# One fused comparison in the dilation, and later transposes in the first GraphSAGE layer

## The chip, the cores and the metric

The kernel runs on one core of one Trainium2 chip. The metric is the device time of one execution in microseconds, as the median of several runs. In the views of the profile PE is TensorE (PEld its weight loads), DVE is VectorE, ACT is ScalarE, POOL is GpSimd and SP is SyncE, which here only issues DMAs.

## What is computed

Two graph layers, each on `relu(layernorm(x))` and added back to x, for B = 16 graphs of N = 1024 nodes with D = 128 features and a sparse symmetric adjacency with weights.

The first layer is attention with 8 heads over the neighbours. The second is three GraphSAGE layers over an adjacency that has been dilated first. The dilation goes through the rows in order, and what a row removes is gone for the rows behind it:

```
def step(carry, n):
    row = jnp.take(carry, n, axis=0)
    nbi = row.astype(jnp.int32)
    num = jnp.sum(nbi)
    sf = jnp.where(num > T_DIL, (num + K_DIL - 1) // K_DIL, 1)   # T_DIL = 10, K_DIL = 2
    rank = jnp.cumsum(nbi)
    rm = row & (rank % sf == 0)
    valid = (mask_b[n] != 0) & (num > 1)
    rm = jnp.where(valid, rm, False)
    keep = ~rm
    carry = carry.at[n].set(row & keep)
    carry = carry.at[:, n].set(carry[:, n] & keep)
    return (carry, None)
```

So a row with more than ten neighbours loses those of rank sf and (where there is one) 2 sf, a row of two to ten neighbours loses all of them, and a row of at most one (or a masked one) loses none. Each GraphSAGE layer is

```
deg = jnp.clip(jnp.sum(adj, axis=-1, keepdims=True), 1.0, None)
out = (jnp.einsum('bij,bjd->bid', adj, x) / deg) @ Wr + x @ Wx + b
out = out / jnp.maximum(jnp.linalg.norm(out, axis=-1, keepdims=True), NORM_EPS)
```

followed by relu and a batch norm over all graphs and nodes; the three layers' results go through one last linear map.

## The kernel before, in words

The program has two stages, one after the other. The order of the instructions of PE, ACT and DVE is the order in which the program text issues them; the DMA queues of SP and POOL are ordered by the scheduler.

**Attention, with the dilation beside it** (about 2315 us). Attention is a loop over 256 turns: 16 graphs, two halves c of 512 query nodes, eight blocks m of 128 key nodes. Each turn has two half steps g (four heads each). One half step does, on PE, the scores of the heads (L554 puts in the mask, L560 the products), then the weighted sums of the half step before (L487, L492); on ACT two exponentials over 128x1024 (L598); on DVE two products with the weights of the adjacency over 128x1024 (L603). Around this the turn transposes a piece of the adjacency (L505 on PE, copied by L508 and made a mask by L512 on ACT), and small steps prepare the next graph and conclude the last (L288 to L432).

The dilation is a generator whose pieces are put between the half steps by planned costs (`beside_attention`). It takes eight blocks k of 128 rows, all 16 graphs at a time. Each block first finds, in seven rounds, which neighbours of the diagonal square are removed (L743 to L847). It then has for each row of the block and each graph the number of neighbours, from which it makes per row the thresholds `th` (L851 to L865). At the end of the block comes a loop over the graphs, `for i in range(B + 2)` (L896), with one graph entering at each i, and its steps set apart by one i each. In this text "row" means one graph of this loop: a tile of 128 rows by 1024 columns. For one graph it does

- i: the sums of pairs along the row on DVE (L900), kept once for two columns, then on ACT two activations `wr = |2 sum + at|` (L915), one for the even and one for the odd columns, each 128x512 in f16, with `at_even` or `at_odd` as a bias per partition;
- i + 1: on DVE, a column is removed where `wr == off`, and everywhere if `allof` says that the row loses all (L924, two operations of 512 columns that write every second column of `er`), times the row (L928); then the removals found by earlier blocks are put in (L930, over the columns before the block);
- i + 2: on PE eight transposes of `er` (L907), copied on ACT (L909); ACT reads the next block's row of this graph (L699, L703); DVE joins the diagonal square (L937) and takes the removed columns out of the next block's row (L716, over the columns before the block); SP writes rows and columns of the removals `mr_d` to HBM and loads `ad`, `gm` and `gl` for later rows.

One graph takes two half steps of attention. The buffers are `wr` 2, `er` 3, `et` 2, `pair_sums` 2.

**GraphSAGE** (from about 2315 us). A loop over three layers L, 16 graphs b and two halves c. A turn reads its half of the transposed adjacency (`aT`, 2 MB) and the removals (`mr`) that were fetched some turns ahead, and DVE has put the one into the other (L146) during the turn before. On PE it does the nodes' own part (L1118), then four pieces "sums" of 16 records each (L1132), into one PSUM tile. The result of the turn before is finished between these pieces: DVE scales it (L1150), ACT squares it (L1155), DVE and ACT make the norm, DVE the normalised `o` (L1165), PE transposes `o` (L1169), ACT copies the transposed tile (L1173), DVE takes the statistics (L1176). Where the transposes stand is set by `turn_later` (L1288): without it they come after the second of the four pieces, with it after the third. In the kernel before it holds for the first halves (c = 0) but the first one of a layer; the second halves (c = 1) have the transposes after the second piece.

Of the kernel before, what the change touches and what calls it, by code (L numbers as in the profile page):

```python
# [34 lines left out]
def swept(ctx: ExitStack, tc: tile.TileContext, t: dict, out: bass.AP, flag: bass.AP):  # L35
# [131 lines left out]
    def first_part(p1):  # L167
# [483 lines left out]
        def dilation():  # L651
# [9 lines left out]
            def rk(b, lo, hi):  # L661
                return rks[b // (B // 2)][:, b % (B // 2), lo:hi]
# [73 lines left out]
            for k in range(NB):  # L736
# [112 lines left out]


                th = small.tile([P, 5, B], F32, name=f"th_{k}", tag="th", bufs=2)  # L851
                num, at_odd, off, allof, at_even = (th[:, i, :] for i in range(5))
                high = v[:, 3, :]
                nc.vector.tensor_tensor(mosts, most, gone[:, B : 2 * B], ALU.subtract)
                nc.vector.tensor_tensor(num, mosts, gone[:, :B], ALU.subtract)
                nc.vector.tensor_tensor(changed[:, k * B : (k + 1) * B], num, prev, ALU.not_equal)
                nc.vector.tensor_scalar(high, num, 10.5, None, ALU.is_gt)
                nc.vector.scalar_tensor_tensor(allof, num, 1.5, high, ALU.is_gt, ALU.subtract)

                nc.vector.tensor_scalar(num, num, 0.5, 0.25, ALU.mult, ALU.add)  # L860
                nc.vector.tensor_scalar(num, num, MAGIC, MAGIC, ALU.add, ALU.subtract)
                nc.vector.tensor_scalar(at_odd, num, -3.0, None, ALU.mult)
                nc.vector.tensor_scalar(at_even, num, -3.0, 2.0, ALU.mult, ALU.add)
                nc.vector.scalar_tensor_tensor(off, num, 1.0, high, ALU.add, ALU.mult)
                nc.vector.tensor_scalar(off, off, -1.0, None, ALU.add)  # L865
                yield 2.0, 1

                nc.vector.tensor_tensor(in_pairs(valid), in_pairs(valid), over_rows(vb[:, 0]), ALU.mult)
# [27 lines left out]
                for i in range(B + 2):  # L896
                    b = i
                    if b < B:
                        row = rk(b, 0, N + 2)
                        nc.vector.tensor_tensor_scan(  # L900
                            pair_sums[b % 2], row[:, 0::2], row[:, 1::2], 0.0, ALU.add, ALU.add
                        )
                    b = i - 2
                    if 0 <= b:
                        pe = ps_d.tile([P, NB, P], BF, name=f"pe_{k}_{b}", tag="d")
                        for j in range(NB):
                            nc.tensor.transpose(pe[:, j, :], ers[b][:, j * P : (j + 1) * P], ident_bf)  # L907
                        ets[b] = pool.tile([P, NB, P], BF, name=f"et_{k}_{b}", tag="et", bufs=2)
                        nc.scalar.copy(ets[b], pe)  # L909
                    yield (1.3 if i < B else 0.0), "B"  # L910
                    b = i
                    if b < B:
                        wrs[b] = pool.tile([P, N], F16, name=f"wr_{k}_{b}", tag="wr", bufs=2)
                        for t, at in enumerate((at_even, at_odd)):
                            nc.scalar.activation(  # L915
                                wrs[b][:, t * HN : (t + 1) * HN], pair_sums[b % 2][:, t : t + HN], AF.Abs,
                                bias=at[:, b : b + 1], scale=2.0,
                            )
                    b = i - 1
                    if 0 <= b < B:  # L920
                        er = ers[b] = pool.tile([P, N], BF, name=f"er_{k}_{b}", tag="er", bufs=3)
                        wr = wrs.pop(b)
                        for t in range(2):
                            nc.vector.tensor_scalar(  # L924
                                er[:, t::2], wr[:, t * HN : (t + 1) * HN], off[:, b : b + 1], allof[:, b : b + 1],
                                ALU.is_equal, ALU.max,
                            )
                        nc.vector.tensor_tensor(er, er, rk(b, 2, N + 2), ALU.mult)  # L928
                        if k > 0:
                            nc.vector.tensor_tensor(er[:, :n0], er[:, :n0], gms.pop(b)[:, :n0], ALU.max)  # L930
                    known(i + 1)
                    b = i - 2
                    if 0 <= b:
                        if more:
                            read(k + 1, b)
                        er, et = ers.pop(b), ets.pop(b)
                        nc.vector.tensor_tensor(er[:, n0:n1], er[:, n0:n1], et[:, k, :], ALU.max)  # L937
                        nc.sync.dma_start(mr_d[b][:, k, :n1], er[:, :n1])
                        if k > 0:
                            nc.sync.dma_start(mr_d[b][:, :k, n0:n1], et[:, :k, :])  # L940
                        if more:
                            nc.sync.dma_start(mr_d[b][:, k + 1 :, n0:n1], et[:, k + 1 :, :])
                            if b >= 2:
                                survive(k + 1, b - 2)
                            fetch_removed(k + 1, b)
                    if more and i < B:
                        fetch(k + 1, i)
                    yield (2.9 if i < B else 1.2), ("A" if i < B + 1 else 1)
# [263 lines left out]
    with tc.manual_schedule(  # L1212
# [6 lines left out]
        for L in range(3):  # L1219
# [10 lines left out]
            for b in range(B):  # L1230
# [4 lines left out]
                for c in range(2):  # L1235
# [49 lines left out]
                            next(last_rows)  # L1285
                    if biased:
                        next(biased)
                    turn_later = before and c == 0 and b > 0  # L1288
                    if before and not turn_later:
                        go(before, "transposed")  # L1290
                    pieces[2]()
# [686 lines left out]
```

## Time and profile before

| what | value |
|---|---|
| median of 3 runs | 3405.87 us (3404.3 to 3407.48) |
| the profiled execution, its own time | 3404.63 us |
| its span, first to last instruction | 3402.8 us |
| mean granted clock of TensorE | 0.994 |
| PE, DVE, ACT busy | 97%, 89%, 68% of the span |
| DVE L603, products of attention | 1024 of 1219 ns |
| ACT L598, exponentials | 1024 of 1022 ns |
| DVE L900, pair sums | 128 of 1218 ns |
| ACT L915, `wr` | 256 of 730 ns |
| ACT L909, copies of the transposed removals | 128 of 994 ns |
| PE L1132, sums of GraphSAGE | 6144 of 275 ns |

A line of the profile's groups reads: line, engine, operation, written tile <- read tiles, shapes, count | busy time in us, mean of one in ns | idle time of the engine just before them, and what ended it. The timeline reads: start and duration in us, engine, line and operation, tiles and count; in brackets the idle time before it, and what ended that. A duration runs from an instruction's start to its end, and consecutive instructions of an engine overlap at their ends, so two of 1022 ns can take 1.94 us together. PE's records are pipelined, so that PE's idle time shows best as the distance between the starts of records.

### The profile page before, as it was taken

The numbers are of one execution on the slowest core, as the hardware profiler recorded it, in microseconds if no ns is written. First come the engines' busy times: TensorE is split into PE (matmuls) and PEld (weight loads), VectorE is DVE, ScalarE is ACT, GpSimd is POOL, SyncE is SP. The second block draws the span as 40 slices with busy tenths as digits, with TensorE's granted clock in tenths as the row PEclk, the third lists the DMA queues.
The fourth block names the chain that finished last, engine by engine and source line by source line (L and its number), as shares of the span: only waits on it lengthen the run. The fifth ranks groups of instructions, "written<-read, shape, count | busy, mean of one in ns | idle before, by whom it ended". The sixth has DMA issues, their size and how long they took to land. (4 is left out here: it accounts for less than half of the span.)

```text
span 3402.8 us, 86338 instructions
## 1 busy us (share of the span) xinstructions
PE 3312.8 (97%) x34855; PEld 1874.3 (55%) x34855; DVE 3023.9 (89%) x5399; ACT 2303.8 (68%) x3909; POOL 163.8 (5%) x253
## 2 busy tenths in 40 slices
PE   8999999999999999999999999999999899999997
PEld 3333333333333333333333334337999899999997
DVE  7898989989989999998998999997888799978887
ACT  7699689779879869968977986883222344423334
POOL 2000000000000000000000000000000000000000
PEclk9999999999999999999999999999999999999999
DMA  7357457547637646845854874677999799989996
GB/s 241 109 169 207 134 151 212 151 138 223 179 121 222 207 128 195 238 126 166 247 175 125 250 221 123 198 230 272 336 334 336 273 354 351 354 308 351 352 351 220
DMA packets 650123, 772.28 MB, mean 227 GB/s; under 512 B 173264, under 2 KB 569168, under 8 KB 637424
## 3 DMA queue, kind: packets, MB, share of 16 engines
q1 hardware_dynamic: 632672, 708.58, 64.3%
q0 software_dynamic: 15456, 57.30, 5.0%
q8 instruction: 275, 4.51, 0.6%
q14 instruction: 136, 1.11, 0.1%
q10 hardware_dynamic: 1584, 0.79, 0.1%
HBM read 508.50 MB, written 157.29 MB: 196 GB/s over the span
## 5 line engine op out<-in xcount | busy, mean ns | idle before, releaser
L603 DVE TENSOR_TENSOR w<-e,aT 128x1024 f32<-128x1024 f32 x1024 | 1205.4, 1219 | 136.4 <-ACT e L598 134.7
L598 ACT ACTIVATE e<-sc 128x1024 f32<-128x1024 f32 x1024 | 991.6, 1022 | 330.0 <-PE sc L560 329.8
L1132 PE MATMUL pg<-y,aT 128*128 128x128 f32 (+1 forms) x6144 | 732.2, 275 | 0.0
L1132 PEld LDWEIGHTS pg<-y,aT 128*128 128x128 f32 x6144 | 710.4, 192 | 0.0
L487 PE MATMUL acc<-w,both 128*32 128x512 f32 x4096 | 586.8, 605 | 1.2 <-DVE w L603 0.8
L560 PE MATMUL sc<-qT,kT 32*128 32x512 f32 x4096 | 584.1, 640 | 0.3 <-ACT qT L315 0.3
L492 PE MATMUL acc<-e,eps 128*32 128x512 f32 x4096 | 573.5, 592 | 0.0
L146 DVE SCALAR_TENSOR_TENSOR aT<-mr,aT 128x1024 f32<-128x1024 bf16 x384 | 458.9, 1217 | 0.0
L492 PEld LDWEIGHTS acc<-e,eps 128*32 128x32 f32 x4096 | 150.6, 110 | 294.6 <-issue 289.3
L1155 ACT ACTIVATE sq<-o 128x512 f32<-128x512 f32 x96 | 60.6, 631 | 357.8 <-DVE o L1150 357.8
L554 PEld LDWEIGHTS <-never 32*32 32x32 bf16 x8192 | 80.1, 88 | 344.3 <-issue 324.0
L554 PE MATMUL sc<-nomask,never 32*32 32x512 bf16 x8192 | 248.6, 385 | 16.0 <-ACT e L598 13.2
L1173 ACT COPY hT<-pt 128x512 f32<-128x512 f32 x96 | 56.2, 585 | 267.7 <-PE pt L1169 259.2
L560 PEld LDWEIGHTS sc<-qT,kT 32*128 32x128 f32 x4096 | 160.1, 183 | 116.9 <-issue 116.1
L505 PEld LDWEIGHTS pa<-ident,a 128*128 128x128 f32 x1024 | 107.8, 141 | 181.3 <-issue 131.2
L487 PEld LDWEIGHTS acc<-w,both 128*32 128x32 f32 x4096 | 92.9, 108 | 154.2 <-issue 65.1
L915 ACT ACTIVATE wr<-both,th 128x512 f16<-128x512 f16 x256 | 172.0, 730 | 7.1 <-DVE both L900 6.9
L505 PE MATMUL pa<-ident,a 128*128 128x128 f32 x1024 | 168.3, 287 | 6.6 <-DMA a<-in_adj 6.0
L512 ACT ACTIVATE nomask<-aT 128x512 bf16<-128x512 f32 x256 | 161.3, 630 | 8.1
L1150 DVE SCALAR_TENSOR_TENSOR o<-pg,rdeg,mine 128x128 f32<-128x128 f32 x384 | 108.2, 345 | 60.1 <-PE pg L1132 57.0
L900 DVE TENSOR_TENSOR_SCAN both<-rk 128x513 f16<-128x513 bf16 x128 | 155.9, 1218 | 0.0
L508 ACT COPY aT<-pa 128x512 f32<-128x512 f32 x256 | 152.8, 597 | 4.5 <-PE pa L505 4.5
(228 smaller groups left out, 3894.0 us busy)
## 6 DMA issues: line engine op xcount, KB each, us to landing
aT<-aT_d SPq DMA_DIRECT2D x94, 2048.0 KB, 9.8
mr<-mr_d SPq DMA_DIRECT2D x188, 512.0 KB, 6.0
aT_d<-aT SPq DMA_DIRECT2D x256, 256.0 KB, 4.0
a<-in_adj SPq DMA_DIRECT2D x253, 256.0 KB, 3.9
ad<-in_adj SPq DMA_DIRECT2D x112, 512.0 KB, 4.2
nomask<-nomask SPq DMA_DIRECT2D x512, 96.0 KB, 2.7
nomask<-nomask SPq DMA_DIRECT2D x512, 64.0 KB, 2.8
nomask<-nomask SPq DMA_DIRECT2D x512, 32.0 KB, 2.7
```

What stands on the lines that cost most here:

```text
L146: nc.vector.scalar_tensor_tensor(part, mrs[h][:, j : j + 2, :].rearrange("p j n -> p (j n)"), 0.0, part, ALU.is_equal, ALU.mult)
L487: nc.tensor.matmul(acc[g][32 * j : 32 * j + 32, :], v1[:, m, (2 * j + g) * HW : (2 * j + g) * HW + 32], ws[j // 2][:, j % 2, :], start=(m ...
L492: nc.tensor.matmul(acc[g][32 * j : 32 * j + 32, :], eps8, es[j // 2][:, j % 2, :], start=False, stop=(m == NB - 1),)
L505: nc.tensor.transpose(pa[:, k * P : (k + 1) * P], a[:, k, :], ident)
L512: nc.scalar.activation(nomask[:, 0, :], aT[:, 0, :], AF.Relu, bias=1.0, scale=-1e38, accum_out=zeros[:, i : i + 1])
L554: nc.tensor.matmul(scs[j // 2][to : to + 32, j % 2, :], never[rows, rows], nomask[rows, j, :], start=True, stop=False, tile_position=(32 * ...
L560: nc.tensor.matmul(scs[j // 2][:, j % 2, :], kT[rows, mm], qTs[c][rows, g, :], start=False, stop=True, tile_position=(32 * j, 0),)
L598: nc.scalar.activation(e, scs[q], AF.Exp, scale=1.0 / math.sqrt(HD))
L603: nc.vector.tensor_tensor(w, es[q], aT.to_broadcast([P, 2, HN]), ALU.mult)
L900: nc.vector.tensor_tensor_scan(pair_sums[b % 2], row[:, 0::2], row[:, 1::2], 0.0, ALU.add, ALU.add)
L915: nc.scalar.activation(wrs[b][:, t * HN : (t + 1) * HN], pair_sums[b % 2][:, t : t + HN], AF.Abs, bias=at[:, b : b + 1], scale=2.0,)
L1132: nc.tensor.matmul(pg[:, i // 2, at : at + width], aT[:, j, i * P : (i + 1) * P], y[:, j, :width], start=(j == 0), stop=(j == NB - 1),)
```

## The change

Two independent parts, one in the dilation and one in the GraphSAGE loop.

In the dilation the two comparisons and the product with the row become one `scalar_tensor_tensor`: `(wr == off) * row`, over both halves, read and written with a step of two elements. The maximum with `allof` is gone. A row that loses all its neighbours is made to compare equal everywhere instead: a new threshold `twos` is 2 for the others and 0 for such a row, it becomes the scale of the two activations (a column of 128 values where the constant 2 was), and `at_odd`, `at_even` and `off` are made from it, so that such a row has `wr = 0 = off`. The thresholds take one small operation more per block.

In the GraphSAGE loop `turn_later` holds for the second halves of the first layer (L = 0) too.

```diff
-                num, at_odd, off, allof, at_even = (th[:, i, :] for i in range(5))
+                num, at_odd, off, twos, at_even = (th[:, i, :] for i in range(5))
...
-                nc.vector.scalar_tensor_tensor(allof, num, 1.5, high, ALU.is_gt, ALU.subtract)
+                nc.vector.scalar_tensor_tensor(twos, num, 1.5, high, ALU.is_gt, ALU.subtract)
+                nc.vector.tensor_scalar(twos, twos, -2.0, 2.0, ALU.mult, ALU.add)
...
-                nc.vector.tensor_scalar(at_odd, num, -3.0, None, ALU.mult)
-                nc.vector.tensor_scalar(at_even, num, -3.0, 2.0, ALU.mult, ALU.add)
+                nc.vector.scalar_tensor_tensor(at_odd, num, -1.5, twos, ALU.mult, ALU.mult)
+                nc.vector.tensor_tensor(at_even, at_odd, twos, ALU.add)
                 nc.vector.scalar_tensor_tensor(off, num, 1.0, high, ALU.add, ALU.mult)
-                nc.vector.tensor_scalar(off, off, -1.0, None, ALU.add)
+                nc.vector.scalar_tensor_tensor(off, twos, -0.5, off, ALU.mult, ALU.add)
...
-                                bias=at[:, b : b + 1], scale=2.0,
+                                bias=at[:, b : b + 1], scale=twos[:, b : b + 1],
...
-                        wr = wrs.pop(b)
-                        for t in range(2):
-                            nc.vector.tensor_scalar(
-                                er[:, t::2], wr[:, t * HN : (t + 1) * HN], off[:, b : b + 1], allof[:, b : b + 1],
-                                ALU.is_equal, ALU.max,
-                            )
-                        nc.vector.tensor_tensor(er, er, rk(b, 2, N + 2), ALU.mult)
+                        nc.vector.scalar_tensor_tensor(
+                            er.rearrange("p (i t) -> p t i", t=2), wrs.pop(b).rearrange("p (t i) -> p t i", t=2),
+                            off[:, b : b + 1], rk(b, 2, N + 2).rearrange("p (i t) -> p t i", t=2),
+                            ALU.is_equal, ALU.mult,
+                        )
...
-                    turn_later = before and c == 0 and b > 0
+                    turn_later = before and (c == 0 or L == 0)
```

## Prediction

> **What bounds the kernel now.** I read the page's busy shares first, then the busy time by stretch, then the timeline inside two of the stretches, then the GraphSAGE stage. The page says that TensorE is the engine that is never free:
>
> ```profile
> PE 3312.8 (97%) x34855; PEld 1874.3 (55%) x34855; DVE 3023.9 (89%) x5399; ACT 2303.8 (68%) x3909; POOL 163.8 (5%) x253
> ```
>
> So an engine beside it matters only where it makes TensorE late, and the change touches two such places.
>
> The first is the part of the dilation that writes the removed pairs, sixteen rows (one per graph) in each of eight blocks. I took its stretches from the first and last pair scan (L900) of each block and asked for the busy time in each. Columns: start:end, length, busy time of PE, PEld, DVE, ACT, POOL (instructions), clock, DMA.
>
> ```profile
> core 0: us, PE busy (x) PEld busy (x) DVE busy (x) ACT busy (x) POOL busy (x), PEclk, DMA share, GB/s
> 178.00:310.00 132.00, 129.13 (x1410) 47.47 (x1403) 118.49 (x188) 130.12 (x228) 4.86 (x6) 1.00 0.65 188
> ...
> 1005.00:1140.00 135.00, 131.14 (x1427) 48.23 (x1423) 128.84 (x211) 132.11 (x231) 5.00 (x6) 1.00 0.72 211
> ...
> 1848.00:1990.00 142.00, 136.48 (x1441) 50.01 (x1434) 136.39 (x211) 132.42 (x204) 4.96 (x6) 1.00 0.80 234
> 2135.00:2265.00 130.00, 127.52 (x1424) 46.73 (x1412) 122.86 (x169) 114.90 (x167) 6.49 (x10) 1.00 0.71 215
> ```
>
> The eight lengths are 132, 132, 133, 135, 137, 140, 142 and 130 us, for about fifteen rows each. The rows grow longer with the block although the attention beside them does not change: what grows is VectorE's work on the columns before the block (L930 and L716). In the early blocks ScalarE has no idle time (130.12 of 132), in block 6 VectorE is as full as it gets. The timelines say the same. First two lines from block 1, then one from block 6:
>
> ```profile
> 546.23 2.36 DVE L603 TENSOR_TENSOR w<-e,aT 128x1024 f32<-128x1024 f32 x2 [0.72 <-ACT e L598]
> 547.16 0.41 PE L554 MATMUL sc<-nomask,never 32*32 32x512 bf16 x8 [0.51 <-ACT e L598]
> ```
>
> ```profile
> 1927.58 0.62 PE L907 MATMUL pe<-ident_bf,er 128*128 128x128 bf16 x8 [0.38 <-DVE er L930]
> ```
>
> In block 1 both VectorE and TensorE wait for ScalarE; in block 6 the transposes of the finished row (L907) wait for VectorE. So VectorE's time is worth something in late blocks only, and ScalarE's time costs in the early ones.
>
> The second place is layer 0 of GraphSAGE, where 32 records of the sums (L1132) come before the transposes (L1169). Two turns in order:
>
> ```profile
> 2392.79 3.74 PE L1132 MATMUL pg<-y,aT 128*128 128x129 f32 x32
> 2396.37 0.60 PE L1169 MATMUL pt<-ident,o 128*128 128x128 f32 x4
> ...
> ```
>
> ```profile
> 2401.48 3.74 PE L1132 MATMUL pg<-y,aT 128*128 128x129 f32 x32
> 2405.35 0.66 PE L1169 MATMUL pt<-ident,o 128*128 128x128 f32 x4
> ```
>
> The first pair is the sequence that is already "later": 3.58 us from start to start, no wait. The second is the one that the change moves: 3.87 us, so 0.29 us of waiting for the normalised o (L1165). The same pattern repeats through the layer.
>
> **VectorE, the fused comparison.** Removed per row: two tensor_scalar and one tensor_tensor.
>
> ```profile
> L924 DVE TENSOR_SCALAR er<-wr,th 128x512 bf16<-128x512 f16 x256 | 132.0, 571 | 0.0
> L928 DVE TENSOR_TENSOR er<-er,rk 128x1024 bf16<-128x1024 bf16 x128 | 88.7, 693 | 4.4
> L315 ACT ACTIVATE qT<-pq,bq,own 128x512 f32<-128x512 f32 x64 | 46.4, 787 | 1.0 <-PE pq L312 1.0
> L324 ACT ACTIVATE kT<-pk,bk 128x512 f32<-128x512 f32 x32 | 22.2, 693 | 1.7 <-PE pk L322 1.7
> ```
>
> In block 6's timeline L924 starts at 1934.24, L928 at 1935.32 and the next step L930 at 1936.05: 1.81 us. Added: one scalar_tensor_tensor over 1024 elements with steps of two. No row has just that form. From below, the 693 ns of L928, if the fused form ran as fast as the 16-bit product. From above, the 2279 ns that the scan L756 needs for 1024 elements. The nearest rows are L146 (the same operation over 1024 elements, 1217 ns) and L716 (the same operation in bf16, 1084 ns for 896), and L924, which already writes at a step of two, takes 571 ns for 512, no more than its share of 1217 ns. I take 1.22 us. Saving: 1.81 - 1.22 = 0.59 us a row, 8.8 us in a stretch of fifteen rows, 75 us of VectorE in all 128.
>
> The Trainium skill speaks against this part: "VectorE: DVE Perf Modes", section "The perf-mode tier table (the rule you actually need)", lets a 16-bit tensor_scalar run four elements a cycle and a tensor_tensor two, and gives no fast mode for the fused form. From its 693 ns at 2048 elements an estimate for L924 is some 0.29 us, so the three removed would be worth 1.27 us, the fusion would save next to nothing, and the sum would be near 3415 us. The row L924 says 571 ns, twice that, so I follow the trace.
>
> The fused step waits for both halves of wr, where the first tensor_scalar waited for one. In block 1 the second half ends at 543.30 and L924 began at 543.00, so the step would wait some 0.5 us; behind it on VectorE stand L930, L937, L716 and the next products L603, and the transposes L907 wait for them. VectorE has that much idle time there; in block 6 (wr done at 1933.45, step at 1934.24) there is no wait.
>
> The thresholds' edits (L855 to L865) add one 128x16 operation a block, 0.17 us by the row of L865. That is 1.4 us in all, in a stage where VectorE waits for counts; I cost it at nothing, 1.4 us if that cover is gone.
>
> **ScalarE, scale from a column.** The activation of L915 gets a scale per partition instead of the constant 2. L324 (bias per partition) against L315 (bias and scale per partition), both over 128x512 f32 out of PSUM: 693 and 787 ns, 0.094 us for the operand. Bounds: zero, if the f16 form takes it for nothing, and 0.094. I take 0.094: two a row, 0.19 us, 2.8 us a stretch, 24 us in all 128 rows. It lies on the path wherever ScalarE is full.
>
> **Sum for the dilation.** Two estimates. (a) The growth of the stretches over block 0 (0, 0, 1, 3, 5, 8, 10 us) is VectorE's; the saving takes back at most 8.8 of each, 0+0+1+3+5+8+8.8 = 25.8. Block 7 has no reading of a next block, so ScalarE is not full there; I give it 2.5 us, its PE idle time (130 - 127.52). ScalarE's 2.8 us is added in seven stretches, 19.6. Net 25.8 + 2.5 - 19.6 = 8.7 us gained. (b) ScalarE as the floor: its busy time (130.12, 129.33, 130.18, 132.11, 132.94, 133.72, 132.42) plus 2.8 plus the 1.9 us of idle time that even block 0 has gives 134.8, 134.0, 134.9, 136.8, 137.6, 138.4, 137.1, against the old lengths +2.8, +2.0, +1.9, +1.8, +0.6, -1.6, -4.9, in sum +2.6; with block 7's -2.5 nothing is gained. (b) counts ScalarE's overlapping ends as work, (a) forgets what couples the engines. I take **5 us gained**, between them.
>
> **The later turn in layer 0.** The order by engine shows 16 sums records more ahead of the transposes in the 16 second halves; ScalarE's and VectorE's orders do not move there, as their steps already stood behind. Sixteen records are 1.79 us (half of 3.58), more than the 0.29 us. Fourteen regular turns give 14 x 0.29 = 4.1 us. The first and the last such turn wait longer:
>
> ```profile
> 2336.21 3.74 PE L1132 MATMUL pg<-y,aT 128*128 128x129 f32 x32
> 2342.57 0.63 PE L1169 MATMUL pt<-ident,o 128*128 128x128 f32 x4 [2.63 <-issue]
> ```
>
> ```profile
> 2343.20:2346.60 3.40, 3.40 (x19) 3.40 (x18) 3.37 (x8) 0.58 (x1) 0.00 (x0) 0.50 0.95 362
> ```
>
> ```profile
> 2643.47 3.74 PE L1132 MATMUL pg<-y,aT 128*128 128x129 f32 x32
> 2648.32 0.63 PE L1169 MATMUL pt<-ident,o 128*128 128x128 f32 x4 [1.11 <-DVE o L1165]
> ```
>
> The first: 6.36 - 3.58 = 2.78 us, of which the 1.79 us of sums now hide as much, and 1.0 us stays. Behind that wait the granted clock is 0.50 for 3.4 us (the windows row), which cost half, 1.7 us; after the 1.3 us wait at 2648 no such drop follows, so with 1.0 us left I expect none. The last: 4.85 - 3.58 = 1.27 us, all of it. Sum 4.1 + 1.8 + 1.7 + 1.3 = **8.9 us gained**. Bounds: 4.1, if the first and the last turn's chains through VectorE only move on, and 8.9. VectorE's bn_stats (L1176) waits some 0.1 us longer at 2407.5; behind it stand the o of the next turn, which need the fourth sums, ready later. SP's order changes only in the place of some loads of ad, two issues later; their landing is 4 us, a row ahead of use, so nothing.
>
> **Rivals.** (A) VectorE's saving is worth more: estimate (a) holds and the smaller waits for er in blocks 2 to 4 go as well, 9 to 18 us; with the turns, as a median, 3379 to 3388. For it: L907 waits for er in every block. Against it: ScalarE's 0.19 us a row comes at the same place. (B) ScalarE eats the saving: estimate (b), and of the turns only 4.1: 3404.6 - 4.1 + 1.2 = 3402 as a median, 3406 if its time counts in block 7 and the rows beside the stretches too (24 us in place of 19.6). (C) Slower: ScalarE decides all blocks. If its time added in every row (24 us) and the stretches were long for ScalarE's sake, not VectorE's, the turns would cover 8.9 of it: 3404.6 + 24 - 8.9 + 1.2 = 3421. It decides from the point where ScalarE's added time in a stretch (2.8 us) is more than what VectorE gave back there; blocks 0 to 3 are past that point by the windows, 4 to 6 are not, since L907 waits for er in them. (D) The fused step runs at the scan's pace, 2.28 us: +0.47 us a row in place of -0.59. In blocks 2 to 6, where VectorE is full, 5 x 15 x 0.47 = 35 us, ScalarE's part lies under it: 3404.6 + 35 - 8.9 + 1.2 = 3432. Against it stand L146 and L716.
>
> **How the numbers follow.** The profiled execution took 3404.6 us (span 3402.8, 1.8 around it); the median of the runs is 3405.87, 1.2 more. 3404.6 - 5 - 8.9 = 3390.7, as a median **3392**. About 0.2% (7 us) is what a measurement of this kernel can tell from no change: faster means under 3399. Chances: forecast (3388 to 3399) 0.55, A 0.21, B (from 3399 up) 0.16, C 0.05, D 0.03. So faster 0.76, same 0.16, slower 0.08. The range 3378 to 3407 takes in A and B and leaves out C, D and a little of each end of A.
>
> **What would show it.** L924 and L928 gone, one row of 1.22 us in their place; L915 at about 820 ns; the stretches of blocks 0 to 2 longer by 1 to 3 us and those of 5 and 6 shorter by 2 to 6; no wait for L1165 ahead of L1169 in layer 0, and no half clock near 2343. Wrong if the fused row is near 2 us, if L915 stays at 730 ns (then A), or if the early stretches grow and the late ones do not shrink.

## The result, and the profile after

The changed kernel takes 3415.5 us, median of 8 runs (3410.1 to 3419.2), beside 3405.3 us (3402.4 to 3407.5, 8 runs) for the kernel before: ratio 1.0029, 95% interval 1.0018 to 1.0040. It is slower by 10 us, and the forecast was 13 us faster. Its profiled execution took 3416.9 us, with a span of 3415.1 us.

The page of the changed kernel gives the busy shares, and VectorE has indeed less to do (2987.3 us against 3023.9), ScalarE more (2323.8 against 2303.8):

```profile
PE 3322.1 (97%) x34855; PEld 1874.4 (55%) x34855; DVE 2987.3 (87%) x5151; ACT 2323.8 (68%) x3909; POOL 169.9 (5%) x253
```

To see where the time went I cut the span at events that both traces have: in each block of the dilation from the first pair scan to the last transpose of the removals ("rows"), from there to the next block's first scan ("between", where the search for removals and attention run), and all after the last block's rows ("rest"). Each figure is a sum of eight stretches, from the traces; the first stretch of all is set apart, because it is the start of the program and differed by up to 3 us from kernel to kernel without regard to their code.

| | start | between (7) | rows (8) | rest | span |
|---|---|---|---|---|---|
| before | 174.5 | 870.4 | 1235.1 | 1122.8 | 3402.8 |
| changed | 176.7 | 886.3 | 1238.2 | 1113.9 | 3415.1 |
| difference | +2.2 | **+15.9** | +3.1 | -8.9 | +12.3 |

So GraphSAGE gave what was forecast, 8.9 us in these two traces; the rows, where the fused step works, gave nothing; and the loss lies between the rows, in a stage that the change does not touch.

**The two steps that the diff names.** The groups of the changed kernel (line, engine, operation, tiles, shapes, count, then busy us and mean ns):

```profile
L916 ACT ACTIVATE wr<-both,th 128x512 f16<-128x512 f16 x256 | 195.5, 823 | 3.3 <-DVE both L901 3.3
L923 DVE SCALAR_TENSOR_TENSOR er<-wr,th,rk 128x1024 bf16<-128x1024 f16 x128 | 177.1, 1383 | 0.0
```

ScalarE's activation went from 730 to 823 ns, as reckoned. The fused step takes 1383 ns where 1220 was reckoned. What counts is from its start to that of the next step; the timeline of the changed kernel in block 6 has

```profile
2020.04 1.39 DVE L923 SCALAR_TENSOR_TENSOR er<-wr,th,rk 128x1024 bf16<-128x1024 f16 x1
2021.46 0.56 DVE L929 TENSOR_TENSOR er<-er,gm 128x768 bf16<-128x768 bf16 x1
```

1.42 us in place of 1.81, so 0.39 us a row is saved and not 0.59.

**GraphSAGE.** The first moved turn, in the timeline of TensorE (48 records of sums now stand ahead of the transposes):

```profile
2357.36 5.52 PE L1131 MATMUL pg<-y,aT 128*128 128x129 f32 x48
2363.71 0.63 PE L1168 MATMUL pt<-ident,o 128*128 128x128 f32 x4 [0.83 <-issue]
...
2370.51 0.66 PE L1085 MATMUL ht<-ident,h0in 128*128 128x128 f32 x4 [1.05 <-ACT h L1087]
...
2419.78 5.53 PE L1131 MATMUL pg<-y,aT 128*128 128x129 f32 x48
2425.14 0.60 PE L1168 MATMUL pt<-ident,o 128*128 128x128 f32 x4
```

In the first pair 6.35 us lie from start to start, where a turn without a wait has 5.36 (the last pair): 1.0 us of the old 2.8 is left, and no half clock follows (granted clock 1.00 from 2360 to 2372 us). A wait of 1.05 us for ScalarE follows (the middle line), which the kernel before does not have.

**What is late between the rows.** The waits of TensorE and VectorE (us in all, times, longest), first of the kernel before, then of the changed one:

```profile
PE sc L554 <- DMA nomask<-nomask: 0.8, 3, 0.3
DVE rk L716 <- DMA gl<-mr_d: 0.5, 1, 0.5
```

```profile
PE sc L554 <- DMA nomask<-nomask: 5.6, 11, 0.9
DVE rk L716 <- DMA gl<-mr_d: 10.0, 7, 2.8
```

All 10.0 us of the waits for gl and 3.6 us of those for nomask lie between the rows, where the kernel before has 0.5 us and none. Both are transfers of SP's queue: `nomask` is the mask of an attention turn, of which SP moves six rotated pieces (L516, L517), and `gl` the removals that the next block's row must lose (L710). Neither is touched by the diff. The timeline of the changed kernel shows both kinds, shortly after a block's rows:

```profile
901.43 0.59 SPq L517 DMA_DIRECT2D nomask<-nomask  x1
...
902.36 0.73 PE L554 MATMUL sc<-nomask,never 32*32 32x512 bf16 x13
...
903.66 0.39 PE L554 MATMUL sc<-nomask,never 32*32 32x512 bf16 x3 [0.57 <-DMA nomask<-nomask]
```

```profile
1186.76 0.69 DVE L716 SCALAR_TENSOR_TENSOR rk<-rk,gl 128x512 bf16<-128x512 bf16 x1 [1.01 <-DMA gl<-mr_d]
...
1187.38 2.36 DVE L603 TENSOR_TENSOR w<-e,aT 128x1024 f32<-128x1024 f32 x2
...
1188.66 0.62 PE L487 MATMUL acc<-w,both 128*32 128x512 f32 x2 [0.64 <-DVE w L603]
```

The last piece of a mask is issued 0.93 us before TensorE begins with that mask, and the records that need it wait until it has landed. The late gl holds up L716, behind it on VectorE the products L603, and behind those TensorE.

**Why SP is late.** In each row SP issues most often 14 transfers (12 to 17; the expectations say 15 or 16), mostly at 0.3 to 0.65 us each, in order. Of them, gl reads what the row's last write (L942, L941 after) has just put into HBM, so SP stands before gl until that write has landed. The timeline of SP, one row of the kernel before and one of the changed kernel:

```profile
1139.12 1.06 SPq L942 DMA_DIRECT2D mr_d<-et  x1
1140.28 0.45 SPq L683 DMA_DIRECT2D ad<-in_adj  x1
1140.83 0.39 SPq L893 DMA_DIRECT2D gm<-mr_d  x1
1141.31 0.38 SPq L938 DMA_DIRECT2D mr_d<-er  x1
1141.86 0.32 SPq L710 DMA_DIRECT2D gl<-mr_d  x1
```

```profile
1151.70 0.49 SPq L941 DMA_DIRECT2D mr_d<-et  x1
1152.29 0.50 SPq L894 DMA_DIRECT2D gm<-mr_d  x1
1152.89 0.39 SPq L937 DMA_DIRECT2D mr_d<-er  x1
1153.87 0.32 SPq L710 DMA_DIRECT2D gl<-mr_d  x1
1154.28 0.38 SPq L683 DMA_DIRECT2D ad<-in_adj  x1
```

In the first, ad is issued in the time in which gl cannot go yet. In the second ad stands behind gl: SP waits 0.59 us with nothing to do (1153.28 to 1153.87) and then spends 0.4 us on ad, and all six pieces of the mask come that much later. 36 of the 112 loads of ad changed their places, 29 of them from ahead of a gl to behind it; besides them six loads of gm and three of a moved. SP's waits for the landing write are 66.5 us before and 80.4 after.

In 2 of the 256 turns of the kernel before, and in 24 of the changed one, the last piece of the mask is issued less than 3 us ahead of its use.

### The profile page after: what moved, and what is told of

Read it like the earlier page. It is cut to its first block, busy times and chain, and to the rows that moved or that the text cites. A ratio compares the mean times of both kernels' runs of the same rounds, so it can differ in the third digit from the quotient of the medians.

```text
span 3415.1 us, 86125 instructions
## 1 busy us (share of the span) xinstructions
PE 3322.1 (97%) x34855; PEld 1874.4 (55%) x34855; DVE 2987.3 (87%) x5151; ACT 2323.8 (68%) x3909; POOL 169.9 (5%) x253
## 5 line engine op out<-in xcount | busy, mean ns | idle before, releaser
L603 DVE TENSOR_TENSOR w<-e,aT 128x1024 f32<-128x1024 f32 x1024 | 1205.7, 1219 | 186.0 <-ACT e L598 183.6
L487 PE MATMUL acc<-w,both 128*32 128x512 f32 x4096 | 574.6, 605 | 3.0 <-DVE w L603 2.3
L492 PE MATMUL acc<-e,eps 128*32 128x512 f32 x4096 | 560.8, 592 | 0.0
L146 DVE SCALAR_TENSOR_TENSOR aT<-mr,aT 128x1024 f32<-128x1024 bf16 x384 | 458.8, 1217 | 0.0
L554 PE MATMUL sc<-nomask,never 32*32 32x512 bf16 x8192 | 275.0, 385 | 35.5 <-ACT e L598 26.7
L554 PEld LDWEIGHTS <-never 32*32 32x32 bf16 x8192 | 89.7, 88 | 381.1 <-issue 354.2
L916 ACT ACTIVATE wr<-both,th 128x512 f16<-128x512 f16 x256 | 195.5, 823 | 3.3 <-DVE both L901 3.3
L923 DVE SCALAR_TENSOR_TENSOR er<-wr,th,rk 128x1024 bf16<-128x1024 f16 x128 | 177.1, 1383 | 0.0
```

What stands on the lines that cost most here:

```text
L146: nc.vector.scalar_tensor_tensor(part, mrs[h][:, j : j + 2, :].rearrange("p j n -> p (j n)"), 0.0, part, ALU.is_equal, ALU.mult)
L487: nc.tensor.matmul(acc[g][32 * j : 32 * j + 32, :], v1[:, m, (2 * j + g) * HW : (2 * j + g) * HW + 32], ws[j // 2][:, j % 2, :], start=(m ...
L492: nc.tensor.matmul(acc[g][32 * j : 32 * j + 32, :], eps8, es[j // 2][:, j % 2, :], start=False, stop=(m == NB - 1),)
L554: nc.tensor.matmul(scs[j // 2][to : to + 32, j % 2, :], never[rows, rows], nomask[rows, j, :], start=True, stop=False, tile_position=(32 * ...
L603: nc.vector.tensor_tensor(w, es[q], aT.to_broadcast([P, 2, HN]), ALU.mult)
L916: nc.scalar.activation(wrs[b][:, t * HN : (t + 1) * HN], pair_sums[b % 2][:, t : t + HN], AF.Abs, bias=at[:, b : b + 1], scale=twos[:, b : ...
```

## The experiments

Theory Q: the new order of SP's queue makes the loss between the rows. Rival E: ScalarE's 93 ns and the later fused step make it, whatever the order. In the table, gl and nomask are the two waits above, in us; the ratio is to the kernel before on the same chip. The expectations count the stretches between the rows otherwise: 1215 and 1236 us run from each block's last pair scan to the next block's first, with the start and 55 us behind the last block; 1045 and 1063 us are the start and "between" of this table together.

| kernel | median | ratio, 95% interval | between (7) | rows | gl | nomask |
|---|---|---|---|---|---|---|
| before | 3405.3 | | 870.4 | 1235.1 | 0.5 | 0.8 |
| changed | 3415.5 | 1.0018 to 1.0040 | 886.3 | 1238.2 | 10.0 | 5.6 |
| turns_only | 3390.6 | 0.9952 to 0.9978 | 870.2 | 1235.4 | 0.5 | 1.1 |
| turns_again | 3398.9 | 0.9974 to 0.9993 | 873.0 | 1235.4 | 2.8 | 1.2 |
| changed_old_queue | 3399.4 | 0.9974 to 0.9993 | 876.8 | 1237.4 | 5.2 | 2.1 |
| before_new_queue | 3415.6 | 1.0020 to 1.0043 | 882.4 | 1237.3 | 7.7 | 5.3 |
| before_only_ad_moved | 3418.4 | 1.0030 to 1.0065 | 882.4 | 1243.2 | 8.0 | 7.2 |
| before_others_moved | 3408.3 | 0.9999 to 1.0017 | 873.0 | 1236.1 | 1.3 | 2.1 |
| scale_only_old_queue | 3415.3 | 1.0023 to 1.0047 | 874.7 | 1246.4 | 3.6 | 3.3 |
| scale_const_old_queue | 3388.2 | 0.9938 to 0.9971 | 875.3 | 1224.2 | 3.8 | 1.7 |
| wr_interleaved_old_queue | 3412.7 | 1.0015 to 1.0034 | 874.7 | 1252.4 | 3.4 | 1.8 |
| changed_ad_on_gpsimd | 3431.6 | 1.0059 to 1.0093 | 883.2 | 1267.4 | 8.4 | 16.2 |
| turns_ad_on_gpsimd | 3435.2 | 1.0073 to 1.0108 | 882.1 | 1263.4 | 6.9 | 9.9 |
| changed_gl_later | 3407.6 | 1.0000 to 1.0019 | 880.4 | 1237.5 | 12.8 | 1.2 |
| turns_gl_later | 3397.4 | 0.9971 to 0.9990 | 871.7 | 1235.1 | 3.0 | 1.0 |
| turns_gl_on_gpsimd | 3398.0 | 0.9971 to 0.9990 | 874.5 | 1236.0 | 2.9 | 0.9 |
| fused_without_column | 3394.4 | 0.9950 to 0.9977 | 883.0 | 1225.6 | 5.1 | 3.5 |

The stretches and waits are from one trace of each kernel. turns_only and turns_again are the same program, and theirs differ by 2.9 us between the rows and by 2.3 us in the waits for gl: differences of this size tell nothing.

**The later turn alone**, twice: the one line `turn_later = before and (c == 0 or L == 0)` put into the kernel before. SP's order is the same with it.

> The kernel before with the later turn of layer 0 as the only change; the orders of all queues and of VectorE and ScalarE stay as they were. Both theories: the 8.9 us that the GraphSAGE stage gained in the changed kernel's trace are this line's alone, so the median falls by 8.9 us to 3396 (3395 to 3398), with the stage until 2320 us unchanged within 1 us. If it gains less than 5 us, a part of the stage's gain came from the rest of the change.

> The later turn of layer 0 alone once more, beside the version without the column on the same chip. Layer 0 was 331.3 us before and 323.0 after, 8.3 us, and the first run of this kernel stood 13.6 us under the kernel before, with its other runs spread over 11 us. If the 8.3 us are all: 3404.5 - 8.3 = 3396 (3394 to 3398). If the first measurement holds: 3390.6 (3389 to 3392).

Layer 0 went from 331.3 to 323.0 us in both traces, 8.3 us. The medians stand 13.6 and 6.8 us under the kernel before, on either side of that and both outside what was expected; the last section says what may have moved them.

**The order of the queue, exchanged.** Edges that set only the order of issue (no wait on a landing) put SP's transfers into a given order; the other engines' orders stayed as they were.

```diff
+    for a, b in zip(SP_ORDER, SP_ORDER[1:]):
+        tc.add_manual_dep(sent[b], sent[a].name, mybir.DependencyInfo(NoSync, DATA), reason="pin")
```

> The changed kernel, all engines' orders as in it, but the loads and stores of SP's queue issued in exactly the order of the kernel before (order edges only, no added waits). Theory Q (the queue's order): the 21 us that the changed kernel lost between the row stretches come from loads of ad put behind the load of gl, which waits for its block's writes to land; SP, which issues 15 or 16 transfers in each row, then brings the rotated masks late. With the old order this loss goes: 3415.5 - 21 = 3394.5 (3392 to 3399), and the eight stretches between rows add up to 1215 us as before, not 1236. Rival E (the engines): ScalarE's 0.19 us more per row and the later fused step make the copies et, the writes of the removals and so the masks late, whatever the order: 3415 (3411 to 3417), stretches still 1236.

> The kernel before, with SP's queue in exactly the order of the changed kernel and nothing else changed. Theory Q: the loss comes without any change of the computation: 3405.3 + 21 = 3426 (3415 to 3428; less than 21 where the rows themselves still give the queue time to catch up), with waits of L554 for nomask of 3 to 4 us in the waits of TensorE, against 0.8 us. Rival E: 3405 (3403 to 3407), waits for nomask at 0.8 us.

The changed kernel with the old queue is 16.2 us faster than with its own (3415.5 to 3399.4, in two measurements), 16.6 us by the spans of the two traces. But 5.5 of the 16.6 us lie in the rest (1113.9 against 1108.4), of which 2.8 us are the beginning of layer 2 (last section); with the new order alone the rest is no longer than before (1121.2 us in before_new_queue, 1122.8 before). Up to the last rows the old order gives back 11 us. The kernel before, with nothing changed but the order of SP, is as slow as the changed kernel: 11.4 us by the medians on one chip, and by the traces 12.0 us between the rows. So theory Q holds for most of the loss, and the order's price is some 11 us by either exchange (between the rows alone 9.5 and 12.0 us by the traces). Rival E is not empty: with the old queue 6.4 us stay between the rows (876.8 - 870.4), some 3 of which two traces of one program can differ by, and gl still comes late, 5.2 us in all.

**Which part of the order.** The same edges, in the kernel before, with only ad in its new places, and with all the others.

> The kernel before with only the loads of ad in the places that they have in the changed kernel's queue of SP (some 36 of 112 are moved, nearly all from ahead of the load of gl to behind it); all other transfers keep the old order. Theory A (ad ahead of gl filled the wait of gl for the write of its row; behind gl the wait is bare and everything behind is later): most of the 11 us that the kernel before lost with the whole new order, 3404.5 + 7 to 11 = 3411 to 3416, waits of L554 for nomask 3 to 5 us and of L716 for gl 4 to 8 us. Rival O (the few others that moved, gm of the first graphs and pieces a of the adjacency, make the loss): 3402 to 3408.

> The complement: the kernel before with the other transfers that moved (six loads of gm, three of a) in the changed kernel's places, and ad in the old ones. Theory A: 3402 to 3408, as before. Rival O: 3411 to 3416.

The waits of the kernel before with only ad moved:

```profile
PE sc L554 <- DMA nomask<-nomask: 7.2, 11, 1.7
DVE rk L716 <- DMA gl<-mr_d: 8.0, 6, 2.9
```

Ad alone makes the whole loss, 12.8 us by the medians; the other moves make 2.7 us, in an interval that touches 1. The loss is the place of 36 loads.

**ScalarE's part and VectorE's.** In scale_only_old_queue, whose queue is not pinned in spite of its label, the kernel before takes its scale from a column of twos:

```diff
+                nc.vector.memset(twos, 2.0)
...
-                                bias=at[:, b : b + 1], scale=2.0,
+                                bias=at[:, b : b + 1], scale=twos[:, b : b + 1],
```

> The kernel before with only the scale of the two activations of wr taken from a column of twos (one memset of 128x16 a block more on VectorE); the three operations of VectorE stay. SP's queue is not pinned here: of 3832 places in it 38 lines differ from the kernel before, against 90 in the changed kernel. ScalarE: the activation goes from 730 to 823 ns, 24 us in all 128 rows. Theory Q: the row stretches grow by 1.5 to 2.8 us each, 12 to 20 us in all, and the stretches between rows by under half of 21 us, for the part of the queue's order that moves: 3405 + 12 to 28 = 3417 to 3433. Rival E: the rows grow as much and the stretches between by the whole 21 us, since ScalarE's delay is what makes the masks late: 3438 to 3446.

3415.3 us, under both bands: the rows grew by 11.3 us where 12 to 20 were expected, the stretches between them by 4.3.

In scale_const_old_queue the changed kernel takes the constant again (and the old queue).

> The changed kernel with SP's queue in the order of the kernel before, and with the constant 2 as the scale of the activations of wr. It leaves out part of the computation: rows that lose all their neighbours are not handled. It tells VectorE's part of the change (three operations in one, 1.38 us) apart from ScalarE's (93 ns more per activation). Theory: of the 8.7 us by which the changed kernel with the old queue (3399.4) stands above the later turn alone (3390.6), all and more is ScalarE's, and VectorE's 0.4 us a row is worth something in the late blocks only (rows that grow by 3 to 8 us there can give up at most 6 each): activations back at 730 ns, 3390.6 - 8 to - 20 = 3371 to 3383. Rival: the fused step, which waits for both halves of wr and starts later, gives the transposes no earlier removals, so its saving is worth nothing: 3389 to 3392. Second rival: the fused step itself costs the 8.7 us: 3397 to 3401.

The rows tell the two apart. Against 1235.1 us, ScalarE's operand alone makes 1246.4 (+11.3), the fused step alone 1224.2 (-10.9), both together 1237.4 (+2.3). VectorE's 0.39 us in each of 128 rows is 50 us of its time and 11 us of the kernel's, by block 0, 0.4, 0.7, 0.8, 1.2, 2.7, 3.5 and 1.4 us: next to nothing where ScalarE is full, most in block 6. ScalarE's 24 us make 11 (alone) to 13 us (1237.4 - 1224.2). The whole came out between the theory and the first rival: of the 11 us won in the rows, 4.9 were lost again between them (875.3 against 870.4), where gl waits 3.8 us.

**The fused step's form.** ScalarE writes wr to every second column, so that VectorE has nothing stepped left:

```diff
-                                wrs[b][:, t * HN : (t + 1) * HN], pair_sums[b % 2][:, t : t + HN], AF.Abs,
+                                wrs[b][:, t::2], pair_sums[b % 2][:, t : t + HN], AF.Abs,
```

> The changed kernel with SP's queue in the order of the kernel before, and with ScalarE writing wr to every second column, so that the fused step of VectorE has no steps of two left: three operands of 1024 elements in a row, f16 and bf16. Theory S (the step of two makes the 1383 ns): the fused step takes 1217 ns as the row L146 of the kernel before, 0.17 us a row less. Rival F (the mixed types make it): it stays at 1383 ns. ScalarE's activation with a stepped f16 output stays at 823 ns or grows, up to the pace of twice that; with 823 ns the time is 3395 to 3400 (0.17 us a row is worth something in the blocks 4 to 6 only, at most 7 us), with every 50 ns more per activation some 6 us more.

The groups of that kernel:

```profile
L916 ACT ACTIVATE wr<-both,th 128x512 f16<-128x512 f16 x256 | 228.5, 971 | 1.1 <-DVE both L901 1.1
...
L923 DVE SCALAR_TENSOR_TENSOR er<-wr,th,rk 128x1024 bf16<-128x1024 f16 x128 | 163.1, 1274 | 0.0
```

Neither theory alone: 109 of the 166 ns above 1217 are the steps of two. The other 57 stay; the types are what is left of the difference from L146 besides the comparison itself, and no run tells the two apart. But ScalarE pays 148 ns more for each stepped output, the rows are 15.0 us longer and the median is 13 us higher for it.

**Out of SP's queue.** The loads of ad by GpSimd (`nc.gpsimd.dma_start` in place of `nc.sync.dma_start` in `fetch`), in the changed kernel and in the kernel with the later turn:

> The changed kernel with the 112 loads of ad issued by GpSimd's queue in place of SP's; nothing else is moved. Theory Q: one transfer in fifteen of a row leaves SP's queue and none of them stands behind the load of gl, so the masks come in time: stretches between the rows from 1063 to 1045 to 1053 us, 3415.5 - 16 = 3399 as with the old order, down to 3391 if the waits that stayed there for gl and nomask go too. Rival: a transfer issued by GpSimd comes later or disturbs VectorE, and the gain is given back: 3410 or more.

> The kernel before with the later turn of layer 0, and the 112 loads of ad issued by GpSimd's queue. Theory Q: the kernel before has 3 waits for masks of 0.8 us in all left, so little is to be had beyond the later turn: 3390.6 - 0 to 3 = 3388 to 3391. Rival: GpSimd's issue disturbs VectorE or comes late: 3394 or more.

A clear miss: 16 us slower than the changed kernel, 36 to 45 slower than the later turn. The theory had thought of the loads as SP's burden, and they had filled a wait. SP's wait ahead of gl, in the queue's own waits of the changed kernel with ad on GpSimd, was 80.4 us and is now

```profile
SPq L710 <- DMA mr_d<-et: 139.7, 103, 3.8
```

What SP no longer issues, it waits. In addition the rows grew by 29 us, and the masks are late there: 12.0 of their 16.2 us of waits lie in the rows. Ad lands in 5.7 us from GpSimd's queue and in 4.4 from SP's; why the masks come later still than with ad on SP was not followed further.

**The wait for gl taken away.** Gl is issued one row later, behind that row's last write (order edges only, the last two rows of a block as before), or by GpSimd:

```diff
-                            nc.sync.dma_start(mr_d[b][:, k + 1 :, n0:n1], et[:, k + 1 :, :])
+                            written = nc.sync.dma_start(mr_d[b][:, k + 1 :, n0:n1], et[:, k + 1 :, :])
+                            with tc.issue_after(written.ins):
+                                if 1 <= b < B - 1:
+                                    fetch_removed(k + 1, b - 1)
...
-                            fetch_removed(k + 1, b)
+                            if b == B - 1:
+                                fetch_removed(k + 1, b - 1)
+                                fetch_removed(k + 1, b)
```

> The changed kernel with the load of gl issued one row later in SP's queue, behind the next row's last write of the removals (the last two rows of a block as before); the loads of ad keep about the changed kernel's places (92 places differ from the kernel before, the places of gl left out). In the runs so far gl stood 2.1 to 2.5 us behind the write that it waits for, and SP waited 0.5 to 0.9 us for it when ad did not stand between; with ad on GpSimd's queue SP waited for gl as much longer (50 to 120 us in all) as the loads of ad had taken, and nothing was won. Theory G (what SP loses is the wait of gl for the write of its row to land): a row later the wait is gone, the masks come in time whatever the order of ad, stretches between rows 1063 to 1045 to 1050 us: 3415.5 - 13 to - 18 = 3398 to 3402. Rival N (SP is full by the number of its transfers, about 16 a row of 0.5 to 0.65 us, and waits do not matter): 3412 to 3417. Rival V: gl now comes late for L716, whose waits grow: over 3417.

> The kernel before with the later turn of layer 0, and the load of gl one row later as above. Theory G: SP's waits for gl go here as well (some 50 us in all rows), but the masks were hardly late (1.5 us of waits): 3390.6 - 0 to 4 = 3387 to 3391. Rival N: 3390 to 3392. Rival V: over 3393.

> The kernel before with the later turn of layer 0, and the load of gl issued by GpSimd's queue, where its wait for the write holds up nothing of attention. It tells whether the 40 us lost with ad on GpSimd's queue come from that queue itself or from ad. Theory: a load on GpSimd's queue lands some 1.5 us later (5.7 against 4.2 us for ad), which gl has: 3387 to 3392. Rival P (what GpSimd issues disturbs the engines): 3400 or more.

SP's wait ahead of gl goes from 80.4 to 10.9 us, and the masks come in time with the changed kernel's own places of ad (waits of 1.2 us in place of 5.6). None of the three bands held: 3407.6 us is 8 us under the changed kernel, so rival N is out, and above theory G's. The stretches between the rows stay 10 us over the kernel before (880.4 against 870.4). What rival V feared shows there, in the waits of VectorE with gl later, against 10.0 us in the changed kernel:

```profile
DVE rk L716 <- DMA gl<-mr_d: 12.8, 9, 3.3
```

In the kernel with the later turn nothing is won, by either way: 3397.4 and 3398.0 us beside 3390.6 and 3398.9 for the later turn alone. Its masks were hardly late. Both expectations started from the 3390.6 us and were missed. Rival P is out: a load on GpSimd's queue does not cost by itself, so the 40 us lost with ad there are ad's.

**The fused step without ScalarE's operand.** A row that loses all gets 49152 added to its bias, where f16 rounds any sum of at most ten neighbours to 49152, and this as `off`:

```diff
+                nc.vector.scalar_tensor_tensor(at_odd, allof, 49152.0, at_odd, ALU.mult, ALU.add)
...
+                nc.vector.scalar_tensor_tensor(off, allof, 49153.0, off, ALU.mult, ALU.add)
...
-                                bias=at[:, b : b + 1], scale=twos[:, b : b + 1],
+                                bias=at[:, b : b + 1], scale=2.0,
```

> A version that computes everything, with the fused step and the later turn, SP's queue in the old order, and without the operand that ScalarE paid for: the scale is the constant 2 again, and a row that loses all gets a bias of 49152 in place of the scale zero, at which f16 rounds every sum of at most ten neighbours to 49152 itself, so that all columns equal off. Two more operations of 128x16 a block on VectorE. If the runs so far are read rightly (ScalarE's 93 ns cost 13 us of the rows, VectorE's saving wins 11 us there and gives 4 back at the end of a block): as the kernel with a constant scale that handled no such rows, 3388 (3385 to 3392), 2 us under the later turn alone. Rival: the constant-scale run gained from what it left out, and this is 3391 or more.

3394.4 us, 0.9963 of the kernel before (0.9950 to 0.9977), and 4.4 us under the later turn alone on the same chip, an advantage that the intervals of the two do not separate. The expected 3385 to 3392 us were missed, and the time lies where the rival had it, but not shown for its reason: the activation is back at 732 ns and the rows are at 1225.6 us, as with the constant scale (1224.2). What differs is the time between them (883.0 us against 875.3). The profiled execution was the slowest of its five runs (3398.2 us), and in it the 9.5 us won in the rows were given back there.

## Why the prediction was wrong, point by point

**The step that failed** is the last sentence of the part on the later turn: "SP's order changes only in the place of some loads of ad, two issues later; their landing is 4 us, a row ahead of use, so nothing." The order was seen, and ad itself is never late. What was not asked is what the two issues are past which ad moved: one of them is gl, which waits, and behind it stand the six pieces of a mask, the last of which was issued 8.1 us ahead of its use in the median of the 256 turns of the kernel before, and 2.1 us in the closest. In place of the forecast "nothing" the experiments show 11 us, by the new order in the kernel before and, up to the last rows, by the old order in the changed kernel. Nor was it only ad: six loads of gm and three of a moved too, for at most 2.7 us. The Trainium skill, "DMA: Bandwidth & Descriptors", section "Anatomy of one DMA — SWDGE (gpsimd) path", states that a transfer's wait for a semaphore happens on the issuing sequencer, before it is dispatched. For SP's queue the gap of 0.59 us ahead of gl, and the 66.5 us (before) to 139.7 us (ad on GpSimd) of such waits, agree.

**The saving of the fused step** was mis-sized: 0.39 us a row, not 0.59 (1383 ns, not 1217). L924 had been read as proof that a step of two costs nothing; in the longer form it costs 109 ns, and another 57 stay beside L146. The sentence on the Trainium skill's "VectorE: DVE Perf Modes" had a sum "near 3415", which is the time that came out, but not by its reason: the three removed steps did take 1.81 us, and the fusion saves VectorE 50 us.

**ScalarE's operand**: 0.094 us reckoned, 93 ns measured, with 11 to 13 us of the kernel.

**The sum for the dilation.** 5 us was taken between the estimates of 8.7 and nothing. From the first to the last scan the eight stretches are 1105 us together in both traces, so it is estimate (b), nothing. The signs by block are as forecast: blocks 0 to 2 grew by 1.9, 1.6 and 1.3 us, blocks 5 and 6 shrank by 1.6 and 2.9. The runs with one part alone show why: VectorE's saving wins 11 us, by block 0 to 3.5, where estimate (a) had up to 8.8 in a block and 28.3 in all, so the growth of the rows over block 0 was not VectorE's alone. ScalarE's operand costs 13 us, 1.7 to 2.2 in each of the blocks 0 to 5, where 2.8 in each of seven blocks were counted.

**The feared wait for both halves of wr** does not show: L923 has 0.0 us of idle time ahead in its 128 rows.

**The later turn** came out near what was worked out: layer 0 is 8.3 us shorter (8.9 forecast), 1.0 us of the first wait is left, no half clock follows it, and a new wait of 1.05 us stands behind it. That the rest of the span is shorter by 8.9 us, the very figure, is in part luck: among the kernels with the later turn the rest goes from 1106.5 to 1113.9 us.

**The thresholds' edits** were costed at nothing; no run prices them alone.

In sum, by profiled executions: 3390.7 was forecast and 3416.9 came, 26.2 us more. By the table of stretches 15.9 us lie between the rows, 8.1 in the rows (3.1 longer, where 5 shorter was forecast), 2.2 at the start, and none in the rest. The queue's order makes 11 us of this: 9.5 between the rows, 0.8 in them, 0.7 at the start. None of the rivals held this case: C, the slower one, had ScalarE decide the rows, and the rows from scan to scan are even.

What stays open: why with the fused step 4 to 13 us stay between the rows although SP's order is the old one (some 3 us can be the spread of the traces). Gl comes late there (3.4 to 5.2 us of waits), and no run shows why. And which rule of the scheduler moves ad, since the diff changes no instruction of SP; with the later turn alone SP's order stays, and with the column of twos alone a part of it moves, so the dilation's part of the diff does it.

## What to carry to other kernels

When a diff moves even a few transfers in an in-order queue, look at what they were standing in front of: a transfer issued while the next one must wait for a landing costs nothing, and behind it costs its issue time to all that follow. Ask of a queue that is full in some stage not when the moved transfer is due, but which one of those behind it is due first, and by how much it leads its use. And a saving on one engine of a chain is worth what it is worth where that engine ends last: here 50 us of VectorE were 11 us, and 24 us of ScalarE 11 to 13.

## What the runs showed of the hardware

Layer 2 of GraphSAGE begins in two ways, whatever the kernel. In four traces (before, changed, turns_only, changed_old_queue) a wait of some 2.54 us is followed by a granted clock of 0.59 to 0.69 over 4 us; in the first two the half clock then goes on, for 10.2 us in all in place of 3.4. The windows of 4 us at this place of the kernel before, then of turns_only (columns as in the prediction, the granted clock is the third figure from the end):

```profile
3004.00:3008.00 4.00, 3.27 (x20) 2.97 (x20) 3.06 (x10) 1.57 (x3) 0.00 (x0) 0.67 0.60 250
3008.00:3012.00 4.00, 3.15 (x13) 2.85 (x14) 4.00 (x15) 1.42 (x3) 0.83 (x2) 0.50 0.33 133
3012.00:3016.00 4.00, 4.00 (x21) 3.85 (x21) 3.95 (x4) 2.06 (x4) 1.31 (x3) 0.55 0.74 252
```

```profile
2994.00:2998.00 4.00, 3.67 (x20) 3.67 (x20) 2.92 (x9) 1.25 (x3) 0.00 (x0) 0.62 0.65 270
2998.00:3002.00 4.00, 3.09 (x24) 2.61 (x23) 4.00 (x16) 2.21 (x4) 0.54 (x1) 0.95 0.24 97
3002.00:3006.00 4.00, 4.00 (x38) 4.00 (x37) 4.00 (x4) 2.01 (x4) 1.60 (x3) 1.00 0.73 251
```

From the end of layer 1 to the start of layer 2 this makes 15.2 us or 12.4; of the seventeen traces nine have the long beginning and eight the short.

Layer 0 has such a choice too. In seven of the twelve traces with the later turn the half clock (3.4 us) comes 8 to 9 us ahead of the first moved turn's transposes, behind a wait of 1.80 us, and layer 0 still takes 323.0 us. The traces of the other five have the same wait and no half clock behind it. Three of the five traces without the later turn have it there as well, and layer 0 takes 1.6 to 1.7 us less in them than in the kernel before. So what the later turn is worth in layer 0 depends on where the half clock falls without it: 8.3 us or some 6.7.

Runs of the kernel before with a mean clock of 0.996 have a median of 3401.8 us (11 runs), those with 0.994 of 3406.7 (37 runs); five of the seven runs of turns_only had 0.996, two of the eleven of turns_again. This goes with one line being worth 13.6 us in one measurement and 6.8 in the next, but it does not show the cause: the traces of these two, one execution each, both have the short beginning and differ by 3.3 us in span, 2.9 of it between the rows. Gains of this size are better read from the stage.
